# Mamba scans issued block by block in a written-out order on all engines, with the layer norm by batch

## The chip, the cores and the metric

The kernel runs on one core of one Trainium2 chip. The metric is device time in microseconds, the median of three executions. A core has five engines that run side by side: TensorE (PE, matmuls), VectorE (DVE, elementwise work and scans), ScalarE (ACT, activations), GpSimd (POOL, elementwise work) and SyncE (SP, which issues most transfers). Each takes its instructions in the order of its own queue, and waits on the others through semaphores.

## The reference, cut to what matters

The input x is 4 x 256 x 32 x 32: batch, channels, and N = 1024 positions. Layer 0 adds to x a block that starts with a group norm, a layer norm over channels, and four Mamba branches of 64 channels each; layer 1 is an attention with a mixture of 16 experts. The change concerns the Mamba branches and what leads to them:

```python
xc = xn.reshape(B, N, NB, DM).transpose(2, 0, 1, 3)          # 4 branches
...
    dA = jnp.exp(dt[..., None] * A)
    dBu = (dt * u)[..., None] * Bm[:, :, None, :]
    def step(h, inp):
        dA_t, dBu_t, C_t = inp
        h = dA_t * h + dBu_t
        return (h, jnp.einsum('bds,bs->bd', h, C_t))
...
    return ys.transpose(1, 0, 2) + u * Dp
...
return y * jax.nn.silu(z) @ outw.T                           # + skip_scale * xc
```

Here u is a short convolution and silu of the branch's input, dt a softplus of a projection of u, and B and C projections of u. Each branch has 128 inner channels with 16 states each, for 4 batches.

## The kernel before, in words

A *unit* is one branch nb in one batch b: 16 units in all. The 128 channels x 16 states of a unit don't fit on 128 partitions, so it is cut into NJ = 16 *blocks* of 8 channels x 16 states, each a tile of 128 partitions x 1024 positions. 256 blocks are scanned.

**The stages.** Part 1 loads the whole of x into four tiles X that stay for the kernel, and all weights. It takes group norm statistics of all batches (L243 to L254), then normalises batch by batch into XM (L260 by groupnorm, L213 to L226 by layernorm, L287). Then come the Mamba units. Part 2 goes over the batches with convolutions, attention, and a projection added to X. Part 3 is the second attention and the routing, part 4 the experts, and part 5 adds their results to X and stores.

**One block** (block j of the current unit `cur`) goes through all engines:

- SyncE spreads 8 rows of dt over 128 partitions into dA (L390), and ScalarE makes exp(dt x A) of it (L391).
- TensorE picks 8 rows of dt x u, spread over 128 partitions, into the PSUM tile dBu (L395). The rows are held as three bf16 parts in U.
- VectorE multiplies dBu by B (L396) and scans it with dA into hs (L398).
- GpSimd multiplies hs by C (L399).
- TensorE sums over the states into the unit's PSUM tile pY (L401).

dBu has two buffers, hs three, dA five, pY one.

**The front** of the next unit makes its u, dt, U, B and C in seven steps (a generator, one step after each block): a convolution as eight matmuls pu (L325) and a silu (L330); a projection pdt (L334) and a softplus as Abs, Relu, Exp, Identity (L339 to L342), a VectorE step (L344), Ln (L345) and a GpSimd step (L346); dt on VectorE (L348), stored to memory (L350), and dt x u on GpSimd (L352); two casts to bf16 on ScalarE (L355, L358), each with a remainder on GpSimd (L356, L359); a store dq (L361); three loads U turned to another layout (L366); and B and C as matmuls pBC (L373) with ScalarE copies (L375). All these matmuls share one PSUM tile with the tag "mm".

**The back** of a unit comes behind its 16 blocks: pz (L408) and its silu (L410), u x D + pY (L412), times silu(z) on GpSimd (L413), the output projection po (L417), and its sum into XM (L418).

The units run with nb outside and b inside. Nothing but the programming layer's scheduler sets the order of instructions on each engine: it may move an instruction ahead of or behind others where data and buffers allow.

Of the kernel before, what the change touches and what calls it, by code (L numbers as in the profile page):

```python
# [8 lines left out]
F32 = mybir.dt.float32  # L9
# [7 lines left out]
N = HH * WW  # L17
# [121 lines left out]
def body(tc, g, out):  # L139
# [8 lines left out]
    with pool("const", 1) as cp, pool("xres", 1) as xp, pool("dram", 1, space=bass.MemoryType.DRAM) as drp:  # L148
# [5 lines left out]


        X = []
        for b in range(B):
            t = xp.tile([P, CT, N], F32, tag=f"x{b}", name=f"x{b}")
            nc.sync.dma_start(out=t, in_=g["x"][b].rearrange("(t p) n -> p t n", p=P))
            X.append(t)  # L160

# [12 lines left out]

        qdw = load("qdw", [P, CT, 3 * NB])
        qpw = load("qpw", [NB, C])
        rpw = load("rpw", [P, CT, C])
        fpw = load("fpw", [P, 2 * CT, C])
        inw = load("inw", [P, CT, 3 * C])
        outw = load("outw", [P, CT, C])  # L180
        fcw = load("fcw", [P, 2 * CT, C])
        projw = load("projw", [P, CT, C])
        wq, wk, wv = (load(n, [P, CT, C]) for n in ("wq", "wk", "wv"))
        gw = load("gw", [P, CT, NE])
        rows = load("rows", [P, 2 * C + NE], g["rows"].partition_broadcast(P))
# [22 lines left out]
        def layernorm(wp, ps, src, dst):  # L208
# [5 lines left out]
            xc = wp.tile([P, CT, N], F32, tag="cm", name="xc")  # L214
            sq = wp.tile([P, CT, N], F32, tag="cm", name="sq")
# [17 lines left out]
        with pool("zero", 1) as zp:  # L233
            zero = zp.tile([P, NE * EROWS * 2 // P], F32, tag="zero", name="zero")
            nc.gpsimd.memset(zero, 0.0)
            nc.gpsimd.dma_start(out=table.rearrange("(p r) c -> p (r c)", p=P), in_=zero)

# [3 lines left out]
        with pool("gn", 2) as gp, pool("gnps", 1, space=PSUM) as gps:  # L241
            for b in range(B):
                nc.vector.tensor_reduce(sums[:, b * CT : (b + 1) * CT], X[b], AX.X, ALU.add)  # L243
            pg = gps.tile([P, B * CT], F32, tag="pg", name="pg")
            mm(pg, grp, sums, start=True, stop=True)
            nc.vector.tensor_scalar(nmean, pg, -1.0, None, ALU.mult)
            for b in range(B):
                for k in range(CT):
                    j = b * CT + k
                    junk = gp.tile([P, N], F32, tag="junk", name="junk")  # L250
                    act(junk, X[b][:, k], AF.Square, bias=nmean[:, j : j + 1], scale=1.0, accum_out=ssq[:, j : j + 1])
            pg2 = gps.tile([P, B * CT], F32, tag="pg2", name="pg2")
            mm(pg2, grp, ssq, start=True, stop=True)
            nc.vector.tensor_copy(gvar, pg2)  # L254
            rsqrt(grstd, gvar, gtmp)

        def groupnorm(dst, b):
            for k in range(CT):
                j = b * CT + k
                ts(dst[k], X[b][:, k], nmean[:, j : j + 1], grstd[:, j : j + 1], ALU.add, ALU.mult)  # L260


        with pool("xm", 1) as xmp:
# [6 lines left out]
            mcs = tc.tile_pool(name="mconst", bufs=1)  # L270
            mc = mcs.__enter__()
            m_in = load("m_in", [P, CT, 2 * DIN], where=mc)
            m_cu = mc.tile([P, CT, K, DIN], F32, tag="m_cu", name="m_cu")
            m_xp = load("m_xp", [DTR, NB, DIN], where=mc)
            m_wdt = mc.tile([P, NB, DIN], F32, tag="m_wdt", name="m_wdt")
            pick = mc.tile([96, 32 // DB, P], BF16, tag="pick", name="pick")
            m_bc = load("m_bc", [P, NB, 2 * P], where=mc)
            m_dt = load("m_dt", [DTR, NB, DIN], where=mc)
            m_out = load("m_out", [P, NB, DM], where=mc)
            with pool("lnA", 2) as wp, pool("lnAps", 2, space=PSUM) as ps:  # L280
                for b in range(B):
                    xs = wp.tile([P, CT, N], F32, tag="xs", name="xs")
                    groupnorm([xs[:, k] for k in range(CT)], b)
                    dst = [XM[b][:, k, XL : XL + N] for k in range(CT)]
                    layernorm(wp, ps, [xs[:, k] for k in range(CT)], dst)
                    for k in range(CT):
                        act(dst[k], dst[k], AF.Identity, bias=V("norm_b", k), scale=V("norm_w", k))  # L287

            aneg = cp.tile([P, NB * DS], F32, tag="aneg", name="aneg")
            act(aneg, V("alog", 0, NB * DS), AF.Exp)  # L290
            ts(aneg, aneg, -1.0, None, ALU.mult)


            with pool("convr", 1) as vp:
                convr = vp.tile([P, CT, K, DIN], F32, tag="convr", name="convr")
                nc.sync.dma_start(out=convr, in_=g["convr"])
                tt(m_cu, m_in[:, :, 0:DIN].unsqueeze(2).to_broadcast([P, CT, K, DIN]), convr, ALU.mult)
                pickf = vp.tile([96, 32 // DB, P], F32, tag="pickf", name="pickf")
                nc.sync.dma_start(out=pickf, in_=g["pick"].rearrange("k (j p) -> k j p", j=32 // DB))
                nc.vector.tensor_copy(pick, pickf)  # L300

            with pool("wdt", 1, space=PSUM) as wps:
                pw = wps.tile([P, NB, DIN], F32, tag="pw", name="pw")
                for nb in range(NB):
                    mm(pw[:, nb], m_xp[:, nb], m_dt[:, nb], start=True, stop=True)
                nc.vector.tensor_copy(m_wdt, pw)
# [4 lines left out]
            NJ = DIN // DB  # L311
            with pool("front", 1) as fp, pool("scan", 3) as sp, pool("dts", 2, space=bass.MemoryType.DRAM) as dsp, pool(
                "mps", 1, space=PSUM
            ) as mps, pool("yps", 1, space=PSUM) as yps, pool("dps", 2, space=PSUM) as dps:
                def block(nb, b):
                    q0 = (nb % 2) * DM
                    return slice(q0, q0 + DM), XM[b][q0 : q0 + DM, nb // 2]

                def front(nb, b, r):

                    rows_in, xb = block(nb, b)
                    pu = mps.tile([P, N], F32, tag="mm", name="pu")
                    for h in HALVES:
                        for k in range(K):
                            mm(  # L325
                                pu[:, h], m_cu[rows_in, nb // 2, k], xb[:, XL - K + 1 + k + h.start : XL - K + 1 + k + h.stop],
                                start=k == 0, stop=k == K - 1,
                            )
                    u = fp.tile([P, N], F32, tag="u", name="u", bufs=2)
                    act(u, pu, AF.Silu, bias=V("convb", nb), scale=1.0)  # L330
                    yield
                    pdt = mps.tile([P, N], F32, tag="mm", name="pdt")
                    for h in HALVES:
                        mm(pdt[:, h], m_wdt[:, nb, :], u[:, h], start=True, stop=True)  # L334


                    e = fp.tile([P, N], F32, tag="e", name="e")
                    dt = fp.tile([P, N], F32, tag="dt", name="dt")
                    act(e, pdt, AF.Abs, bias=V("dtb", nb), scale=1.0)  # L339
                    act(dt, pdt, AF.Relu, bias=V("dtb", nb), scale=1.0)  # L340
                    act(e, e, AF.Exp, scale=-1.0)
                    act(pdt, e, AF.Identity, bias=one, scale=1.0)  # L342
                    yield
                    stt(e, pdt, -1.0, e, ALU.add, ALU.subtract)  # L344
                    act(pdt, pdt, AF.Ln)  # L345
                    nc.gpsimd.tensor_tensor(dt, dt, e, ALU.subtract)  # L346
                    yield
                    tt(dt, dt, pdt, ALU.add)  # L348
                    ds = dsp.tile([NJ, DB, N], F32, tag="ds", name="ds")
                    nc.sync.dma_start(out=ds.rearrange("j d n -> (j d) n"), in_=dt)  # L350
                    dtu = e
                    nc.gpsimd.tensor_tensor(dtu, dt, u, ALU.mult)  # L352
                    yield
                    parts = fp.tile([P, 3, N], BF16, tag="parts", name="parts")
                    nc.scalar.copy(parts[:, 0], dtu)  # L355
                    nc.gpsimd.tensor_tensor(dtu, dtu, parts[:, 0], ALU.subtract)  # L356
                    yield
                    nc.scalar.copy(parts[:, 1], dtu)  # L358
# [594 lines left out]
```

## Time and profile before

The median of three executions is 4861.83 us (4855.08 to 4865.09); the profiled execution spans 4846.0 us.

| stretch | from, us | to, us |
|---|---|---|
| loads, statistics, layer norms, m_cu | 0 | 122 |
| first front and Mamba units | 122 | 1640 |
| part 2 (four batches) | 1640 | about 3530 |
| parts 3 to 5 | about 3530 | 4846 |

Over the span TensorE is busy 78%, VectorE 44%, ScalarE 30%, GpSimd 25%. These shares average over stages with different limits, so the stage itself is to be read. A line of the page's groups names the line, the engine, the operation, the tiles, the busy time, the mean time of one in ns, and behind the second bar the engine's idle time ahead of such instructions with what ended it.

### The profile page before, as it was taken

Reading aid. Unit: us, or ns where it says so; the run is one execution under the profiler, and the core shown is the slowest. Engines: PE = TensorE matmul, PEld = TensorE weight load, DVE = VectorE, ACT = ScalarE, POOL = GpSimd, SP = SyncE. Lnnn points to the kernel's source line nnn. Section 1 sums busy time; section 2 is a strip of 40 time slices with the busy share of each in tenths; the row PEclk is TensorE's granted clock in tenths of the full one; section 3 lists DMA queues with packets and bytes.
Section 4 is the critical chain, followed back from the end, with each engine's and each line's share of the span. In section 5 each row is a group of like instructions: output and inputs, shape, how many; then the busy total and the mean of one; then the engine's idle time right before and its main releaser. Section 6 shows DMA issues by size and latency. Waiting matters only on the chain.

```text
span 4846.0 us, 37340 instructions
## 1 busy us (share of the span) xinstructions
PE 3763.7 (78%) x14694; PEld 2010.7 (41%) x14694; DVE 2145.5 (44%) x2108; ACT 1468.9 (30%) x1864; POOL 1192.6 (25%) x738
## 2 busy tenths in 40 slices
PE   3667776767777699859985998599848776689997
PEld 1222222222222255415541554155425444478885
DVE  3366666666656544344434443544343233311112
ACT  4434434434433033313331333133322112111112
POOL 1354554555544200000000000000010122144441
PEclk8688887878878766866676668666868987799998
DMA  2443443444433000000000000000000000055554
GB/s 88 109 116 105 126 113 100 135 111 109 130 104 104 26 1 1 1 0 1 1 1 0 1 1 1 0 1 1 1 0 9 1 9 9 12 182 184 178 182 161
DMA packets 81831, 292.45 MB, mean 60 GB/s; under 512 B 13998, under 2 KB 18357, under 8 KB 75640
## 3 DMA queue, kind: packets, MB, share of 16 engines
q1 hardware_dynamic: 63272, 194.72, 14.5%
q0 software_dynamic: 18384, 95.36, 6.0%
q8 instruction: 115, 1.88, 0.2%
q14 instruction: 60, 0.49, 0.0%
HBM read 251.68 MB, written 42.27 MB: 61 GB/s over the span
## 4 chain that ended last, share of the span: by engine, by line
PE 60%; DVE 14%; POOL 10%; issue 9%; ACT 5%; DMA 2%; SPq 0%; DVEq 0%; POOLq 0%; ACTq 0%
PE sc L525 10%; PE pY L401 8%; PE pp L543 7%; PE lin L205 6%; PE p L851 6%; POOL hs L399 5%; PE po L553 4%; DVE hs L398 4%; PE po L859 3%; PE pu L325 2%; PE po L662 2%; PE sc L915 2%; PE pv L222 2%; DVE xd L613 2%; PE pm L213 1%
## 5 line engine op out<-in xcount | busy, mean ns | idle before, releaser
L401 PE MATMUL pY<-hs,const 128*128 128x512 f32 x1024 | 632.1, 762 | 180.3 <-POOL hs L399 176.6
L399 POOL TENSOR_TENSOR hs<-hs,bc 128x1024 f32<-128x1024 f32 x256 | 597.7, 2349 | 627.2 <-DVE hs L398 623.0
L525 PE MATMUL sc<-kT,qT 32*128 32x512 f32 x1024 | 575.2, 873 | 37.0 <-ACT pr L531 37.0
L398 DVE TENSOR_TENSOR_SCAN hs<-dA,dBu 128x1024 f32<-128x1024 f32 x256 | 575.5, 2274 | 18.0 <-PE pY L401 10.6
L396 DVE TENSOR_TENSOR dBu<-dBu,bc 128x1024 f32<-128x1024 f32 x256 | 304.6, 1221 | 446.1 <-PE dBu L395 445.9
L391 ACT ACTIVATE dA<-dA,aneg 128x1024 f32<-128x1024 f32 x256 | 292.8, 1147 | 592.0 <-DMA dA<-ds 588.8
L401 PEld LDWEIGHTS pY<-hs,const 128*128 128x128 f32 x1024 | 231.0, 242 | 543.8 <-POOL hs L399 309.9
L528 DVE TENSOR_REDUCE nm<-sc 128x1 f32<-128x1024 f32 x256 | 307.4, 1222 | 286.1 <-PE sc L525 286.1
L543 PEld LDWEIGHTS pp<-const,pr 128*128 128x128 f32 x2048 | 298.8, 177 | 270.4 <-issue 109.0
L226 POOL TENSOR_TENSOR xo<-xc,r 128x1024 f32<-128x1024 f32 x8 | 18.6, 2340 | 1565.9 <-DVE r L198 1565.9
L543 PE MATMUL pp<-const,pr 128*128 128x128 f32 x2048 | 377.9, 345 | 3.4 <-ACT pT L545 2.7
L531 ACT ACTIVATE pr<-sc,nm 128x1024 f32<-128x1024 f32 x256 | 286.3, 1119 | 294.0 <-DVE nm L528 293.9
L851 PE MATMUL p<-xT,w 128*128 128x256 f32 x1504 | 335.6, 381 | 9.5 <-issue 8.7
L395 PE MATMUL dBu<-U,pick 96*128 96x512 bf16 x512 | 165.6, 424 | 183.8 <-DVE hs L398 183.5
L851 PEld LDWEIGHTS p<-xT,w 128*128 128x128 f32 x1504 | 285.1, 191 | 52.4 <-ACT y L864 14.3
L545 DVE COPY pT<-pp 128x512 f32<-128x512 f32 x256 | 175.6, 686 | 231.5 <-PE pp L543 231.5
L545 ACT COPY pT<-pp 128x512 f32<-128x512 f32 x256 | 149.4, 584 | 412.2 <-PE pp L543 412.1
L854 DVE TENSOR_TENSOR hid<-s,p 128x512 f32<-128x512 f32 x94 | 64.6, 687 | 359.9 <-PE p L851 297.1
L525 PEld LDWEIGHTS sc<-kT,qT 32*128 32x128 f32 x1024 | 153.4, 242 | 168.8 <-issue 89.1
L553 PEld LDWEIGHTS po<-pT,v 128*32 128x32 f32 x4096 | 181.8, 167 | 99.0 <-issue 85.2
L553 PE MATMUL po<-pT,v 128*32 128x128 f32 x4096 | 222.0, 406 | 0.0
L859 PE MATMUL po<-w,hid 128*128 128x256 f32 x752 | 181.9, 386 | 0.0
(282 smaller groups left out, 4432.7 us busy)
## 6 DMA issues: line engine op xcount, KB each, us to landing
dA<-ds SPq DMA_DIRECT2D x256, 512.0 KB, 4.5
dq<-parts SPq DMA_DIRECT2D x16, 768.0 KB, 3.5
U<-dq SPq DMA_DIRECT2D x48, 256.0 KB, 5.7
ds<-dt SPq DMA_DIRECT2D x16, 512.0 KB, 2.6
y<-ybuf SPq DMA_DIRECT2D x32, 256.0 KB, 4.2
x<-x SPq DMA_DIRECT2D x4, 1024.0 KB, 10.3
tokens<-out_rows SPq DMA_DIRECT2D x4, 1024.0 KB, 4.5
out<-o SPq DMA_DIRECT2D x16, 256.0 KB, 2.5
```

Of the source, the lines that this page charges most:

```text
L391: act(dA, dA, AF.Exp, scale=aneg[:, nb * NJ + j : nb * NJ + j + 1])
L396: tt(dBu, dBu, cur["B"], ALU.mult)
L398: nc.vector.tensor_tensor_scan(hs, dA, dBu, 0.0, ALU.mult, ALU.add)
L399: nc.gpsimd.tensor_tensor(hs, hs, cur["C"], ALU.mult)
L401: mm(pY[:, h], strip[:, P - DB - j * DB : 2 * P - DB - j * DB], hs[:, h], start=j == 0, stop=j == NJ - 1)
L525: mm(sc[i][:, h], qT[r0 : r0 + HD, k, qs], kT[r0 : r0 + HD, k, h], start=True, stop=True)
L528: nc.vector.tensor_reduce(nm, sc[i], AX.X, ALU.max, negate=True)
L543: nc.tensor.transpose(pp[:, j * P : (j + 1) * P], pr[:, c0 : c0 + P], ident)
L545: (nc.vector.tensor_copy if half == 0 else nc.scalar.copy)(dst, pp)
L553: mm(po[i * HD : (i + 1) * HD], v[:, j, hd * HD : (hd + 1) * HD], pT[j // 4][:, i, (j % 4) * P : (j % 4 + 1) * P], start=j == 0, stop=j == ...
L851: mm(p[:, cc], w[:, o : o + P], xT[:, k], start=k == 0, stop=k == CT - 1)
L859: mm(po[:, h], hid[:, c, h * P : (h + 1) * P], w[:, o : o + C], start=c == 0, stop=c == HID // P - 1,)
```

## The change

Four things are changed, the first two in part 1. They are meant to keep every engine supplied during the scans, and to let the first scan start earlier.

**1. The scans.** The loop over blocks is written out over all 256 blocks, in a region in which each engine keeps the order of the program. In step t: product and scan of block t, times C, dBu of block t + 2, pY of block t - 2, transfer of dA for block t + 4, exponential for block t + 3; and steps of the fronts of the next two units at set places (a table of pairs: step number, function). The back of a unit is put into the next unit: gated at j = 2, project_out at j = 6, store at j = 7; gate (pz and its silu) is at j = 10 of its own unit. hs has four buffers, u three. The units run with b outside.

**2. The start.** Statistics, group norm and layer norm are done batch by batch (normalise). The first front stands behind batch 0, ahead of batches 1 to 3. m_cu and the other small tables are made at the beginning, and the weights of part 2 and later are loaded behind the layer norms.

**3. X.** The tiles X are not held during the Mamba part. x is loaded into three rotating tiles for part 1, and loaded again into X ahead of part 2.

**4. The table of the routing** is zeroed where the routing begins, through SyncE's queue, and not at the start through GpSimd's.

```diff
-        with pool("zero", 1) as zp:
-            zero = zp.tile([P, NE * EROWS * 2 // P], F32, tag="zero", name="zero")
-            nc.gpsimd.memset(zero, 0.0)
-            nc.gpsimd.dma_start(out=table.rearrange("(p r) c -> p (r c)", p=P), in_=zero)
...
+            order = [(nb, b) for b in range(B) for nb in range(NB)]
...
+                    return [(i - 5, lambda i=i: project(i)) for i in range(4)] + [
+                        (-1, silu), (0, project_dt), (1, exps), (3, rest), (4, log), (5, dt_out), (6, times_u),
+                        (8, part1), (8, lambda: spread(0)), (9, lambda: spread(1)), (10, part2), (11, turn),
+                    ]
...
+                    normalise(0)
+                    fronts = [front(n) for n in range(len(order))]
+                    for _, step in fronts[0]:
+                        step()
+                    for i, step in fronts[1]:
+                        if i < 0:
+                            step()
+                    for b in range(1, B):
+                        xs.append(load_x(b))
+                        normalise(b)
...
+                    with tc.manual_schedule():
+                        for t in range(4):
+                            fetch(t)
+                        for t in range(3):
+                            decay(t)
+                        for t in range(2):
+                            select(t)
+                        for t in range(NBLK + 9):
+                            n, j = t // NJ, t % NJ
+                            if t < NBLK:
+                                r = state[n]
+                                dBu = dBus.pop(t)
+                                tt(dBu, dBu, r["B"], ALU.mult)
+
+                                hs = hss[t] = sp.tile([P, N], F32, tag="hs", name="hs")
+                                nc.vector.tensor_tensor_scan(hs, dAs.pop(t), dBu, 0.0, ALU.mult, ALU.add)
+                                nc.gpsimd.tensor_tensor(hs, hs, r["C"], ALU.mult)
+                            if j == 2 and n > 0:
+                                gated(n - 1)
+                            select(t + 2)
+                            add_up(t - 2)
+                            fetch(t + 4)
+                            decay(t + 3)
+                            for ahead in (1, 2):
+                                if n + ahead < len(order):
+                                    for i, step in fronts[n + ahead]:
+                                        if i == j - (ahead - 1) * NJ:
+                                            step()
+                            if n > 0 and j == 6:
+                                project_out(n - 1)
+                            if n > 0 and j == 7:
+                                store(n - 1)
+                            if n < len(order) and j == 10:
+                                gate(n)
...
+            xp = late.enter_context(tc.tile_pool(name="xres", bufs=1, side="right"))
+            X = []
+            for b in range(B):
+                t = xp.tile([P, CT, N], F32, tag=f"x{b}", name=f"x{b}")
+                nc.sync.dma_start(out=t, in_=g["x"][b].rearrange("(t p) n -> p t n", p=P))
+                X.append(t)
...
+            zero = rp.tile([P, NE * EROWS * 2 // P], F32, tag="zero", name="zero")
+            nc.gpsimd.memset(zero, 0.0)
+            nc.sync.dma_start(out=table.rearrange("(p r) c -> p (r c)", p=P), in_=zero)
```

In the new code `select` is the dBu matmul, `add_up` the pY matmul, `fetch` the transfer of dA, `decay` its exponential, `turn` the transfers dq and U, `spread` the matmul and copy of B or C, and `rest`, `log`, `dt_out`, `times_u`, `part1` and `part2` are the steps of the front in their old order.

## The prediction

> **What bounds the kernel now.** I read the page's groups first, then the windows by stage, then the chain of waits and the VectorE timeline inside one turn of the scan loop.
>
> ```profile
> L401 PE MATMUL pY<-hs,const 128*128 128x512 f32 x1024 | 632.1, 762 | 180.3 <-POOL hs L399 176.6
> L398 DVE TENSOR_TENSOR_SCAN hs<-dA,dBu 128x1024 f32<-128x1024 f32 x256 | 575.5, 2274 | 18.0 <-PE pY L401 10.6
> L396 DVE TENSOR_TENSOR dBu<-dBu,bc 128x1024 f32<-128x1024 f32 x256 | 304.6, 1221 | 446.1 <-PE dBu L395 445.9
> 122.00:1640.00 1518.00, 1083.35 (x2113) 391.06 (x2114) 940.79 (x578) 596.74 (x528) 776.54 (x339) 0.81 0.41 111
> ```
>
> The window columns are length, then busy time of PE, PEld, DVE, ACT, POOL, then clock, DMA share and GB/s. The Mamba part takes 1518 us, and no engine fills it: PE 71%, DVE 62%. VectorE sits idle 446 us ahead of the dBu product, waiting for the TensorE matmul that writes dBu. The reader should see a loop of waits, not a full engine.
>
> ```profile
> 602.96 2.29 DVE hs L398
> ...
> 605.38 2.35 POOL hs L399
> ...
> 607.78 6.19 PE pY L401 x8
> 613.96 0.22 PE dBu L395
> 614.18 1.72 PE pY L401 x4
> 615.90 0.23 PE dBu L395
> ...
> 616.15 0.04 DVE dBu L396
> ```
>
> That is the chain of waits: start, duration, piece. From the scan at 602.96 the work goes to GpSimd (times C), to the pY matmuls, and only behind these to the dBu matmuls, which VectorE needs for its next blocks. TensorE's queue order puts dBu of the next blocks behind pY of these ones, so the engines take turns: 618.43 - 602.96 = 15.47 us for three blocks.
>
> ```profile
> 602.96 4.45 DVE L398 TENSOR_TENSOR_SCAN hs<-dA,dBu 128x1024 f32<-128x1024 f32 x2
> 607.33 1.21 DVE L396 TENSOR_TENSOR dBu<-dBu,bc 128x1024 f32<-128x1024 f32 x1
> 608.67 2.29 DVE L398 TENSOR_TENSOR_SCAN hs<-dA,dBu 128x1024 f32<-128x1024 f32 x1
> 616.15 2.36 DVE L396 TENSOR_TENSOR dBu<-dBu,bc 128x1024 f32<-128x1024 f32 x2 [5.20 <-PE dBu L395]
> 663.08 1.23 DVE L396 TENSOR_TENSOR dBu<-dBu,bc 128x1024 f32<-128x1024 f32 x1 [1.74 <-PE dBu L395]
> 664.22 1.21 DVE L348 TENSOR_TENSOR dt<-dt,pdt 128x1024 f32<-128x1024 f32 x1
> 665.35 2.28 DVE L398 TENSOR_TENSOR_SCAN hs<-dA,dBu 128x1024 f32<-128x1024 f32 x1
> 667.54 2.34 DVE L396 TENSOR_TENSOR dBu<-dBu,bc 128x1024 f32<-128x1024 f32 x2
> ```
>
> From this timeline I take the VectorE spacings: a scan starts 1.34 us after the product it needs (607.33 to 608.67); whatever follows a scan starts 2.19 us after it (665.35 to 667.54); an independent elementwise operation takes 1.13 to 1.14.
>
> ```profile
> 568.00:572.00 4.00, 2.29 (x7) 0.97 (x6) 4.00 (x3) 1.96 (x2) 4.00 (x2) 1.00 0.46 131
> 604.00:608.00 4.00, 0.83 (x3) 0.34 (x4) 4.00 (x3) 0.00 (x0) 2.62 (x2) 0.75 0.36 97
> 608.00:612.00 4.00, 4.00 (x5) 1.63 (x6) 2.82 (x2) 1.19 (x2) 2.93 (x2) 0.50 0.67 165
> ```
>
> These short windows show the clock. It stays at 1.00 while TensorE is busy 57% with gaps of 1.7 us; after a pause of 4.2 us (ahead of the dBu matmul at 605.29) it is 0.50. Weight loads in the timeline come every 0.427 us at full clock and 0.853 at half, so a 128x512 f32 matmul (two records) is 0.85 or 1.71 us.
>
> **What the Trainium skill says.** "TensorE: Matmul & The Clock Gate", section "What's actually happening": the clock is halved after an idle window of about 3.4 us and restored after a busy one. The windows above agree. The same page, "Architectural detail: the array is 16× 32×32, not 1× 128×128", says that ScalarE, VectorE and GpSimd run strictly in order, so a waiting instruction holds all behind it; I rely on this below. "ScalarE: Activation LUTs", section "What ACT_TABLE_LOAD costs": 1283 ns plus a drain of about 1380. The trace has the 1283 ns (20.5 us for 16 loads); the exp table load ends at 162.85 and the exponential starts at 162.87, so no further drain is seen and I use 1.28. "DMA: Bandwidth & Descriptors", section "Two DMAs through the same engine are not ordered": a transfer that reads what another writes needs its completion. The trace agrees: U is issued at 166.97, 4.1 us after dq at 162.87.
>
> **The change, part by part.**
>
> *Order of the scans.* A unit is one (nb, b) of 16, with 16 blocks. In the written order TensorE computes dBu two blocks ahead and pY two blocks late. The dBu matmul of block t+2 needs only the end of scan t, which frees its buffer, and has until the end of scan t+1. pY finds its input long ready. So VectorE should run product, scan, product, scan: 1.34 + 2.19 = 3.53 us per block, 256 x 3.53 = 904 us. Per unit it also has the softplus rest (1.13), dt (1.14), gated (1.20 by 626.85 to 628.05) and store (1.32 by 633.26 to 634.58): 4.79, in 15 units 72.
>
> *Can the other engines keep up?* TensorE at full clock: 0.43 (dBu) + 1.71 (pY) = 2.14 us in each block, and in nine of 16 (j = 0, 6, 8 to 14) another 1.71 for a projection: 3.85. Seven such blocks in a row lag 7 x 0.32 = 2.2 us behind VectorE, inside the block of slack that dBu has (3.53 less 0.5). In sum 16 x 2.14 + 9 x 1.71 = 50 us of about 64; gaps are at most 1.4 us, so I take the clock as full. GpSimd: 16 x 2.35 + 3 x 2.35 + 2 x 2.13 = 49. ScalarE: 16 x 1.15 + silus, exps, log, casts, copies (11 operations, 11.6) + six table loads of 1.28 = 38. DMA: 105 to 129 GB/s over units of 95 us becomes about 165 at 64 us; single 4 us windows reach 307. None fills the unit.
>
> *Waits that the order adds on VectorE.* dt (j = 5) is queued ahead of product 6. It needs GpSimd's dt - e, which is queued behind hs of block 4: scan 4's end + 2.35 + 2.35 = 4.7, while VectorE is there after 3.53: 1.2 us. store (j = 7) needs project_out, which ends 0.43 + 1.71 + 1.71 + 0.3 after scan 6: 0.6 us. Each is paid 15 times: 18 and 9 us.
>
> *The turn (j = 11).* SyncE issues dq when GpSimd has parts (scan 10's end + 5.9, since ScalarE waits for spread in j = 8 and 9), waits about 4.1 for its landing, then issues U three times in 1.3; U lands 5.6 later: about 16.2 after scan 10. The first dBu of the next unit is due by scan 15 (5 x 3.53 = 17.7): it fits by about 1 us. Behind U stand the fetches of dA from block 16 on: issued at about 11, landed with 4.5 to 8.1 us behind U's traffic at 16 to 19, exponential 1.15; due at 5 x 3.53 + 1.34 = 19.0. This is between no wait and some 3 us; I take 1.5 a unit, 22 in all. Table loads and the single "mm" buffer make ScalarE late by up to a block, but each step has one or two blocks of slack, the tightest (exps of j = 1 ahead of rest at j = 3) about 0.9 us.
>
> Sum from the first to the last scan: 904 + 72 + 18 + 9 + 22 = 1025 us. The tail: hs 2.4, pY 1.9, gated 1.3, times sz 2.35, po 1.9, store 1.3 = 11.
>
> *The start.* Before, the first scan starts at 185.7: statistics of all batches to 31.8, four layer norms to 119, m_cu at 121, then front 0 alone (122 to 182). Now batch 0 has statistics at about 18 (x lands at about 8, then 2.3 for the sum, 2.3 of squares, some 5 of table loads and small steps) and is normalised 26.6 later, as its first layer norm took from 31.8 to 58.4; front 0 then runs beside batches 1 to 3, which take 20 us each (52.4, 72.5, 92.8 between GpSimd steps): 45 + 60 = 105. For sharing ScalarE (about 75 us of work and loads in this stretch) I add 10. The scan tiles lie in the freed memory, so the first fetch comes at about 115, and 4.5 + 1.15 later the first scan: 122. I take 107 to 150 as ends.
>
> *What costs nothing.* Weight loads move behind the layer norms; SyncE is idle there. X is read again (4 MB): room is free when the last hs is used, some 7 us before the tail ends, and X is first used at 1661.30, 21 us after part 2 begins; a load of 1 MB took 10.3. The zero fill of the table goes from the start to the routing: a 1 us memset and 512 KB, hidden by the attention ahead of the first scatter. Parts 2 to 4 otherwise keep their instructions.
>
> New end of the Mamba part: 122 + 1025 + 11 = 1158, against 1639.7 now: 481 us less. From the median, 4861.8 - 481 = 4380 us.
>
> **The rivals.**
>
> *TensorE at half clock.* If the pattern doesn't hold the clock, each unit needs 16 x 4.27 + 9 x 3.41 = 99 us, TensorE is the bound, and the part ends at 122 + 1584 + 13 = 1719: 79 us later than now, 4941 us. For it: clock 0.81 now. Against it: at half clock TensorE would have no gap, and full windows bring 1.00. This ends on the slower side.
>
> *SyncE's queue becomes the bound.* If U or the dA behind it come 4 to 8 us late per unit instead of 1.5, that is 40 to 100 us more: 4420 to 4480. For it: margins of 1 us in the turn. Against it: four dA are in flight ahead.
>
> *Clock in between (0.8).* TensorE needs 50 / 0.8 = 62 us a unit; its lag beats its slack in the dense blocks, 3 to 6 us a unit: 4430 to 4480.
>
> *No waits at all and a short start.* 107 + 976 + 11 = 1094: 546 less, 4316.
>
> **How the numbers follow.** My forecast (4335 to 4420) has 0.62, SyncE's queue 0.16, a clock in between 0.09, no waits 0.08, half clock 0.04, and 0.01 for a cancelling loss in the rescheduled later parts. The likeliest time is 4380. The range goes down to 4310, for the short start, and up to 4490, for the SyncE and clock cases. Faster by over 0.2% 0.95, within 0.2% 0.01, slower 0.04.
>
> **What would show it.** Scans 3.5 us apart with no wait for dBu; VectorE over 90% busy in the scan stretch; clock 0.95 or more there; first scan near 122, last near 1145; unit length near 64; waits of dt on GpSimd of 1.2 and of store on po of 0.6. Wrong if scans wait for dA after each j = 11, or TensorE shows 0.5 with no gaps, or the first scan comes after 150.

## The result, and the profile after

The changed kernel takes 4451.86 us in the median of four executions (4440.12 to 4459.88), beside 4858.45 us for the kernel before on the same chip. The ratio is 0.9161, with a 95% interval of 0.9136 to 0.9187. The forecast was 4380 us: the gain is 407 us where 481 were worked out. The profiled execution spans 4438.3 us, and its parts are these:

| | before, us | forecast, us | after, us |
|---|---|---|---|
| start of the first scan | 185.7 | 122 | 139.8 |
| from there to the start of the last scan | 1436 | 1023 | 1073.6 |
| end of the last store of the Mamba part | 1639.7 | 1158 | 1228.5 |
| from there to the end of the span | 3206 | 3206 | 3210 |

So the 72 us that are missing are 18 at the start, 51 between the scans, and a few in the rest. The later parts are as long as before, to 4 us. X is loaded again at 1220.21 and first used at 1247.00, with no wait for it.

First the page's groups of the kernel after; behind the first bar stand busy time and mean ns, behind the second the idle time ahead of such instructions and what ended most of it:

```profile
L476 DVE TENSOR_TENSOR_SCAN hs<-dA,dBu 128x1024 f32<-128x1024 f32 x256 | 585.4, 2287 | 81.9 <-PE pY L459 49.7
L459 PE MATMUL pY<-hs,const 128*128 128x512 f32 x1024 | 532.9, 646 | 14.3 <-DVE u L342 12.5
L473 DVE TENSOR_TENSOR dBu<-dBu,bc 128x1024 f32<-128x1024 f32 x256 | 311.6, 1217 | 1.7 <-PE dBu L451 1.6
```

The idle time ahead of the dBu product, 446 us before, is 1.7: the loop of waits is gone. A pY record takes 646 ns, 762 before, since the clock is higher. In place of the old wait stands a smaller one that the forecast had at nothing: the scan waits 49.7 us for pY, which has to release the hs buffer that the scan writes.

The windows of the kernel after (length; busy time of PE, PEld, DVE, ACT, POOL; clock, DMA share, GB/s): the scans, then one stretch of dense blocks (blocks in which TensorE has a projection besides dBu and pY) and two behind pauses of TensorE.

```profile
138.00:1216.00 1078.00, 885.50 (x2055) 343.33 (x2056) 953.18 (x571) 565.36 (x511) 764.63 (x331) 0.93 0.59 153
604.00:608.00 4.00, 4.00 (x11) 1.54 (x10) 3.35 (x3) 0.00 (x0) 3.11 (x2) 1.00 1.04 221
640.00:644.00 4.00, 3.00 (x5) 1.45 (x5) 3.90 (x3) 1.15 (x1) 2.91 (x2) 0.60 0.75 215
651.00:655.00 4.00, 3.34 (x5) 1.48 (x6) 3.87 (x3) 0.00 (x0) 3.25 (x2) 0.51 0.51 124
```

In the scan stretch VectorE is busy 88% (62% before) and the clock is 0.93 (0.81 before). It is 1.00 in the stretch of dense blocks shown, and near a half in the two short ones.

The waits of VectorE in the scan stretch of the kernel after (the instruction that waited, what for; us in total, times, longest):

```profile
DVE hs L476 <- PE pY L459: 49.7, 79, 1.6
DVE xm L356 <- PE mm L350: 29.5, 15, 2.4
DVE dt L292 <- POOL dt L289: 18.5, 15, 1.2
DVE hs L476 <- ACT dA L444: 9.8, 1, 9.8
DVE dBu L473 <- PE dBu L451: 1.6, 3, 0.6
```

Beside hs waiting for pY these are store (L356), waiting for project_out; dt (L292), waiting for GpSimd; one wait of 9.8 for the very first dA, which belongs to the start; and almost nothing for dBu. Three terms make up the stretch from first to last scan. From start to start there are 255 spacings of 3.53 us, 900 us; the extras (the four VectorE operations of a unit that are no part of a block: gated, rest, dt and store) are 72, as forecast; and the waits are 49.7 + 29.5 + 18.5 + 1.6 = 99.3. That makes 1072, against 1073.6 measured. Where the waits come from is seen in TensorE's timeline; the columns are start, duration, engine, line, and in brackets the idle time ahead:

```profile
600.82 0.60 PE L451 MATMUL dBu<-U,pick 96*128 96x512 bf16 x2
601.26 1.88 PE L459 MATMUL pY<-hs,const 128*128 128x512 f32 x4
603.07 1.98 PE L263 MATMUL mm<-xm,m_cu 64*128 64x512 f32 x4
604.98 0.60 PE L451 MATMUL dBu<-U,pick 96*128 96x512 bf16 x2
...
641.00 1.01 PE L451 MATMUL dBu<-U,pick 96*128 96x512 bf16 x2 [3.68 <-DVE hs L476]
641.80 3.10 PE L459 MATMUL pY<-hs,const 128*128 128x512 f32 x4
644.83 1.93 PE L350 MATMUL mm<-u,m_out 128*64 128x512 f32 x4
...
658.61 0.60 PE L451 MATMUL dBu<-U,pick 96*128 96x512 bf16 x2
659.05 1.88 PE L459 MATMUL pY<-hs,const 128*128 128x512 f32 x4
660.76 1.88 PE L320 MATMUL mm<-u,m_bc 128*128 128x512 f32 x4
662.48 0.60 PE L451 MATMUL dBu<-U,pick 96*128 96x512 bf16 x2
```

A dense block with a 128-row projection takes 662.48 - 658.61 = 3.87 us, and the forecast had 3.85. One with the 64-row convolution (L263) takes 604.98 - 600.82 = 4.16, without a gap and at full clock: pY is 1.81 from start to start and the convolution 1.91, where the first has 1.71 and 1.72. Of the seven dense blocks of a unit, five are of the 64-row kind (j = 10 to 14). In the middle, TensorE pauses 3.68 us in the block of j = 5 and runs at half clock behind it, so that the projection that store needs comes late. VectorE's timeline of the same turns:

```profile
607.51 2.29 DVE L476 TENSOR_TENSOR_SCAN hs<-dA,dBu 128x1024 f32<-128x1024 f32 x1 [0.65 <-PE pY L459]
...
611.68 2.29 DVE L476 TENSOR_TENSOR_SCAN hs<-dA,dBu 128x1024 f32<-128x1024 f32 x1 [0.65 <-PE pY L459]
...
636.19 1.22 DVE L292 TENSOR_TENSOR dt<-dt,mm 128x1024 f32<-128x1024 f32 x1 [1.23 <-POOL dt L289]
...
646.80 1.27 DVE L356 SCALAR_TENSOR_TENSOR xm<-xm,vec,mm 64x1024 f32<-64x1024 f32 x1 [2.34 <-PE mm L350]
```

Scans in a row of 64-row blocks are 611.68 - 607.51 = 4.17 us apart, TensorE's pace, with 0.65 of waiting each time. The 79 waits for pY in the list are about five in each of the 16 units, most of them at j = 13 to 15, 0 and 1.

The waits of store show what the clock does. Of the 15, eleven are 2.3 to 2.4 us and four are 0.72 to 0.75, close to the 0.6 of the forecast. One of the four, a unit later (TensorE, then VectorE):

```profile
710.80 0.59 PE L451 MATMUL dBu<-U,pick 96*128 96x512 bf16 x2 [3.27 <-DVE hs L476]
711.23 1.88 PE L459 MATMUL pY<-hs,const 128*128 128x512 f32 x4
...
715.01 1.29 DVE L356 SCALAR_TENSOR_TENSOR xm<-xm,vec,mm 64x1024 f32<-64x1024 f32 x1 [0.75 <-PE mm L350]
```

The same pY takes 1.88 us here and 3.10 at 641.80. Here the half clock came earlier, and was over when TensorE reached the block of project_out, though it had paused 3.27 us ahead of that.

### The profile page after: what moved, and what is told of

Same layout as the page of the kernel before. It is cut to its first block, busy times and chain, and to the rows that moved or that the text cites. A ratio compares the mean times of both kernels' runs of the same rounds, so it can differ in the third digit from the quotient of the medians.

```text
span 4438.3 us, 37207 instructions
## 1 busy us (share of the span) xinstructions
PE 3600.0 (81%) x14706; PEld 1973.7 (44%) x14706; DVE 2176.5 (49%) x2123; ACT 1460.9 (33%) x1872; POOL 1193.8 (27%) x737
## 3 DMA queue, kind: packets, MB, share of 16 engines
q8 instruction: 115, 1.88, 0.2%
## 4 chain that ended last, share of the span: by engine, by line
PE 66%; DVE 15%; POOL 5%; ACT 4%; issue 4%; DMA 2%; SPq 0%; DVEq 0%; POOLq 0%; ACTq 0%
PE sc L606 11%; PE pp L624 7%; PE pY L459 7%; PE p L935 7%; PE lin L188 6%; PE po L634 5%; PE po L943 4%; DVE hs L476 3%; PE po L746 2%; PE sc L999 2%; PE mm L263 2%; PE dBu L451 2%; PE pv L205 2%; DVE xd L694 2%; POOL hs L477 2%
## 5 line engine op out<-in xcount | busy, mean ns | idle before, releaser
L476 DVE TENSOR_TENSOR_SCAN hs<-dA,dBu 128x1024 f32<-128x1024 f32 x256 | 585.4, 2287 | 81.9 <-PE pY L459 49.7
L459 PE MATMUL pY<-hs,const 128*128 128x512 f32 x1024 | 532.9, 646 | 14.3 <-DVE u L342 12.5
L209 POOL TENSOR_TENSOR xo<-xc,r 128x1024 f32<-128x1024 f32 x8 | 18.6, 2340 | 1563.5 <-DVE r L181 1563.5
L459 PEld LDWEIGHTS pY<-hs,const 128*128 128x128 f32 x1024 | 209.2, 206 | 204.0 <-issue 166.8
L451 PEld LDWEIGHTS <-pick 96*128 96x128 bf16 x512 | 42.1, 99 | 381.7 <-issue 303.1
```

Of the source, the lines that this page charges most:

```text
L451: mm(dBus[t][:, h], pick[:, j % 4], state[t // NJ]["U"][:, j // 4, h], start=True, stop=True)
L459: mm(r["pY"][:, h], strip[:, P - DB - j * DB : 2 * P - DB - j * DB], hs[:, h], start=j == 0, stop=j == NJ - 1)
L476: nc.vector.tensor_tensor_scan(hs, dAs.pop(t), dBu, 0.0, ALU.mult, ALU.add)
```

## The experiments

There are three theories on the missing 51 us between the scans: TensorE's pace in the dense blocks, where hs is freed late; SyncE's queue around the turn, the rival of the prediction; and the pauses around dt and store. A fourth question is how much of the gain comes from the order in which instructions are handed out, and how much from holding every engine to it. All times at a glance, with the first-to-last-scan time of each trace:

| kernel | median, us | ratio to before (95%) | first to last scan, us |
|---|---|---|---|
| before | 4858 | 1 | 1436 |
| after | 4452 | 0.9161 (0.9136 to 0.9187) | 1074 |
| e1_dt_late | 4394 | 0.9044 (0.9030 to 0.9058) | 1021 |
| e2_hs6 | 4447 | 0.9153 (0.9132 to 0.9175) | 1072 |
| e3_free_order | 4330 | 0.8913 (0.8863 to 0.8963) | 965 |
| e4_two_taps | 4455 | 0.9172 (0.9146 to 0.9199) | 1091 |
| e5_gate7 | 4383 | 0.9044 (0.9012 to 0.9076) | 1013 |
| e6_split_turn | 4390 | 0.9055 (0.9030 to 0.9081) | 1022 |
| e7_taps_split | 4412 | 0.9093 (0.9056 to 0.9130) | 1045 |
| e8_free_plain | 4766 | 0.9820 (0.9795 to 0.9845) | 1347 |
| e9_three | 4376 | 0.9031 (0.9011 to 0.9051) | 1006 |
| e10_free_front1_late | 4327 | 0.8938 (0.8917 to 0.8959) | 967 |
| e11_between | 4393 | 0.9068 (0.9047 to 0.9090) | 1022 |
| e12_free_dbu_only | 4432 | 0.9137 (0.9111 to 0.9164) | 1045 |

The kernel before was run beside each group of experiments, with medians of 4844 to 4858; so kernels of different groups are compared by their ratios.

**e1: dt one block later.** The step dt_out goes from j = 5 to j = 6.

```diff
-(3, rest), (4, log), (5, dt_out), (6, times_u),
+(3, rest), (4, log), (6, dt_out), (6, times_u),
```

> dt_out moves from j = 5 to j = 6, one block later; the same work. Theory (waits on VectorE, and the pause they give TensorE): the wait of dt on GpSimd (18.5 us in 15 times) goes to about 0; TensorE's pause of 3.7 us at j = 5 shrinks under 3, so its clock stays full and the wait of store on project_out (29.5 us) falls under 5; in sum 40 to 50 us less than the changed kernel's 4452, about 4405. Rival (TensorE's whole work sets the unit's length): what is saved comes back as longer waits of the scan on pY, the time stays within 10 us of 4452.

The waits of VectorE in the scan stretch of e1:

```profile
DVE hs L476 <- PE pY L459: 48.3, 81, 1.1
...
DVE xm L356 <- PE mm L350: 0.7, 1, 0.7
```

The dt wait is gone, and with it all but 0.7 us of the store wait, which the edit doesn't touch: 47 us of waits out, 52 us less from first to last scan. So the two were one. VectorE's block of j = 5 took 3.53 + 1.14 + 1.2 = 5.87 us, and TensorE, with 2.14 of work there, paused for the rest of it, 3.73 (3.68 in the trace), and then ran at half clock. But the clock did not stay full, as the theory had it: between 150 and 1100 us it is 0.95, beside 0.94 in the changed kernel. The half clock has moved to other blocks, away from project_out: in e1 a pause of 2.36 us ahead of 607.10 is followed by a pY of 3.17 us. The waits for pY stay, so they have another cause.

**e2: six hs buffers in place of four.**

```diff
-hs = hss[t] = sp.tile([P, N], F32, tag="hs", name="hs")
+hs = hss[t] = sp.tile([P, N], F32, tag="hs", name="hs", bufs=6)
```

> hs gets six buffers in place of four; the same work. Theory (in blocks j = 8 to 14 TensorE itself needs 4.17 us a block and sets the pace; dBu of the block is due from it almost as early as the buffer): VectorE gains only some 0.4 us a unit, 0 to 10 us in all, and waits for dBu appear where waits for pY were. Rival (too few hs buffers): the 49.7 us of waits of the scan on pY go, 40 to 50 us less.

The scan's waits for pY are gone, and in the waits of VectorE of e2 there stands instead:

```profile
DVE dBu L473 <- PE dBu L451: 32.4, 67, 0.6
```

The time is that of the changed kernel, as the theory had it. The buffers only decide where VectorE waits for TensorE; the pace is TensorE's.

**e4: two of the four taps of the convolution left out.** (A tap is one of the four shifted inputs that are multiplied and summed.) The parts at j = 12 and 14 are then empty, and TensorE has 3.8 us less to do in the dense blocks.

```diff
-for k in range(part % 2 * 2, part % 2 * 2 + 2):
-    mm(..., start=k == 0, stop=k == K - 1)
+for k in range(2) if part % 2 == 0 else ():
+    mm(..., start=k == 0, stop=k == 1)
```

> Leaves out two of the four taps of the convolution (half of the matmuls of pu), so that blocks j = 12 and 14 have no projection on TensorE. Theory (a dense run of seven blocks at 4.17 us against VectorE's 3.54 builds up a lag of 4.4 us, over the slack of about 3): the lag stays under the slack, waits of the scan on pY fall from 50 to under 15, 35 to 45 us less than 4452. Rival (hs buffers or another wait): waits on pY stay over 30.

No gain, where 35 to 45 us were expected, though the waits of VectorE in e4 show that the scan's wait for pY fell from 49.7 to 18.6. From first to last scan e4 is even 17 us longer than the changed kernel; its first scan comes 8 us earlier, at 132.1. The waits:

```profile
DVE u L342 <- PE pY L459: 41.7, 14, 5.9
...
DVE hs L476 <- PE pY L459: 18.6, 30, 0.7
```

A new wait of 41.7 us, of gated (L342) for pY, took its place. Its source is found by following the releasers back. TensorE's timeline in e4, at the first projection of the next unit (project_dt, which needs the silu of u):

```profile
620.04 1.98 PE L274 MATMUL mm<-u,m_wdt 128*128 128x512 f32 x4 [2.22 <-ACT u L267]
```

and ScalarE's ahead of it:

```profile
614.16 1.15 ACT L444 ACTIVATE dA<-dA,aneg 128x1024 f32<-128x1024 f32 x1 [1.08 <-DMA dA<-ds]
616.41 1.15 ACT L444 ACTIVATE dA<-dA,aneg 128x1024 f32<-128x1024 f32 x1 [1.10 <-DMA dA<-ds]
617.58 1.28 ACT L267 ACT_TABLE_LOAD   x1
618.87 1.11 ACT L267 ACTIVATE u<-mm,vec 128x1024 f32<-128x1024 f32 x1
```

The exponentials wait for dA; the silu stands behind them on ScalarE, project_dt behind the silu, and behind project_dt on TensorE the pY that gated needs. The dA stand behind dq and U in SyncE's queue: U is issued at 603.86, and the next dA only at 605.23. So SyncE's queue may be a second limit, right behind TensorE's; e7 tries that.

**e7: e4 with the turn split.** If that is so, the three loads U, which wait for dq to land and hold all behind them, must not be issued at once. The step turn issues dq at j = 11, and a new step back issues U at j = 12, so that a fetch of dA goes between. The two taps are left out here too.

```diff
-(10, part2), (11, turn),
+(10, part2), (11, turn), (12, back),
```

> Leaves out two of the four taps of the convolution, as in the run with two taps, and splits the turn over j = 11 and 12; dt_out at j = 5. Theory (with the dense run thinned, SyncE's queue was what held ScalarE, then project_dt and pY at the unit's start): the wait of gated on pY, 41.7 us, falls under 10, and the time falls to about 4410. Rival (that wait has another source on ScalarE or TensorE): within 10 us of 4455.

Two of the waits of VectorE in e7:

```profile
DVE hs L479 <- PE pY L462: 17.3, 25, 2.3
DVE u L345 <- PE pY L462: 5.4, 2, 4.5
```

Gated's wait (L345 here) for pY fell from 41.7 to 5.4, and first to last scan by 46 us. With two taps left out, then, SyncE's queue was the limit, and what lies between e4 and e7 was its own: 0.9172 - 0.9093 of 4858, or 38 us (two executions each; the intervals don't meet). The dt and store waits are still in e7, since dt_out is at j = 5 in it.

**e6: the split turn on e1, with all taps.** The same edit as in e7, on top of e1's.

> dt_out at j = 6 as before, and the loads of U move from j = 11 to j = 12, behind the transfer of dA of block j + 4, so that this transfer doesn't stand behind the landing of dq. Theory (TensorE's dense run is the binding limit there, the queue of SyncE the next one): ScalarE's 8 us wait for dA shortens, but the time stays within 10 us of 4394. Rival (SyncE's queue sets the unit already): 20 to 40 us less.

4390 beside 4394, and the interval of the ratio covers e1's: no gain that could be told from none. The scan still waits 46.6 us for pY, as in e1. ScalarE's longest wait for dA fell, from 8.1 to 5.5 us, as expected. The edit that frees SyncE's queue paid with two taps and pays nothing here: with the full convolution TensorE is the first limit.

**e5: gate earlier.** pz, one of the 64-row projections, goes from j = 10 to j = 7, out of the dense blocks; on top of e1's edit.

```diff
-if n < len(order) and j == 10:
+if n < len(order) and j == 7:
     gate(n)
```

> dt_out at j = 6 as before, and gate (the pz matmul and its silu) moves from j = 10 to j = 7, so that TensorE's dense run of seven blocks becomes two runs of four. Theory (the dense run's lag makes the waits of the scan on pY, 48 us): each run's lag stays under the slack, the waits fall under 20 us, 20 to 30 us less than 4394. Rival (ScalarE's order: the silu at j = 7 holds the casts of parts behind it, and U comes later): waits move to gated or to dBu at the unit's start, 0 to 20 us more than 4394.

The waits of VectorE in e5:

```profile
DVE u L342 <- PE pY L459: 25.1, 15, 4.5
DVE hs L476 <- ACT dA L444: 21.5, 14, 9.5
DVE hs L476 <- PE pY L459: 2.8, 4, 1.7
```

The wait for pY ahead of the scan is nearly gone (48.3 to 2.8), so it has to do with the run of dense blocks. But the edit does two things: it takes a projection out of the run, and it fills TensorE's pause at j = 7. The clock between 150 and 1100 us is 0.98, beside 0.95 in e1, and the block of j = 8, the first of the long run, takes 3.86 us where it takes 5.58 in most units of e1, at half clock. How the two share the effect was not tried. And as in e4, other waits come forward: gated waits 25.1 and the scans 12 us for dA (9.5 of the 21.5 are the start). First to last scan is 8 us shorter than in e1, where 20 to 30 were expected; the times don't settle it, since the intervals overlap.

**e9: all three, dt late, gate at j = 7 and the split turn.**

> Fixed order with three moves together: dt_out at j = 6, gate at j = 7, the loads of U at j = 12. Theory (with dt and the dense run mended, the queue of SyncE is the last limit: in the run with gate at j = 7, waits of 25 us of gated on pY and of 12 us on dA came from it): these waits fall under 10 in sum, about 4355. Rival (the turn isn't what holds the unit's start): within 10 us of 4383.

The waits of VectorE in e9 (line numbers are 3 higher):

```profile
DVE hs L479 <- PE pY L462: 23.4, 30, 2.1
DVE hs L479 <- ACT dA L447: 9.6, 1, 9.6
DVE dBu L476 <- PE dBu L454: 6.2, 8, 1.4
```

The waits of gated, and those for dA but for the one of the start, are gone. But the scan's waits for pY, 2.8 in e5, are 23.4, half of e1's 48.3; so in e5 the other waits had hidden a part of them. The 4355 expected became 4376. A cause that the waits of VectorE don't show stands in TensorE's own waits, between 150 and 1100 us of e9:

```profile
PE dBu L454 <- DMA U<-dq: 16.3, 13, 3.6
```

With U issued a block later, TensorE itself waits for U at the end of 13 units (9.9 us in e5, none in e1). How much of the 23.4 comes from this was not tried. By its median e9 is the fastest of the kernels that hold the written order, though its interval overlaps those of e1, e5 and e6.

**e11: e9 with the extras between product and scan.** The scan starts 1.34 us after its product, an independent operation after 1.13. So gated, rest and dt_out were put into that place, at j = 2, 4 and 7 (with times_u behind dt_out), to use the 0.2 us.

```diff
 tt(dBu, dBu, r["B"], ALU.mult)
+if j == 2 and n > 0:
+    gated(n - 1)
...
 hs = hss[t] = sp.tile([P, N], F32, tag="hs", name="hs")
```

> The three moves, and gated, rest and dt_out put between a block's product and its scan (at j = 2, 4 and 7), where VectorE has a gap of 0.2 us between the two. Theory: 0.2 us for each of three operations in 15 units, 5 to 15 us less than the run with the three moves. Rival (the operations put there delay the scan and what GpSimd and ScalarE do with their results): the same or up to 20 us more.

The rival came true: e11 is 18 us slower than e9. The largest of VectorE's waits in e11:

```profile
DVE u L345 <- PE pY L462: 36.7, 15, 2.9
```

VectorE comes to gated a scan earlier, before the pY of the unit is summed, and waits for it in all 15 units. A place that saves 0.2 us cost 2.4.

**e3: the written order as a program only.** The region that holds each engine to it is taken away (contextlib.nullcontext() in place of it), and the scheduler may move instructions again. Nothing else differs from the changed kernel.

```diff
-with tc.manual_schedule():
+with contextlib.nullcontext():
```

> The region of fixed order is taken away: the same instructions are emitted in the same order, but the scheduler may move them on each engine. Theory (the order on TensorE's queue is what brought the gain): the scheduler ranks pY and dBu its own way, waits of VectorE on dBu return in part, 4500 to 4750. Rival (emitting dBu two blocks ahead and pY two behind, with b outside, is enough): within 20 us of 4452.

4330 us, about 120 less than the changed kernel, whose interval of the ratio lies wholly above; neither theory nor rival had expected a gain. The four executions lie between 4303 and 4354 us, so the 120 are known to some 25. VectorE's timeline in e3:

```profile
639.49 1.21 DVE L473 TENSOR_TENSOR dBu<-dBu,bc 128x1024 f32<-128x1024 f32 x1
640.60 1.27 DVE L342 SCALAR_TENSOR_TENSOR u<-u,vec,pY 128x1024 f32<-128x1024 f32 x1
641.79 2.28 DVE L476 TENSOR_TENSOR_SCAN hs<-dA,dBu 128x1024 f32<-128x1024 f32 x1
...
652.86 2.34 DVE L473 TENSOR_TENSOR dBu<-dBu,bc 128x1024 f32<-128x1024 f32 x2
655.11 4.46 DVE L476 TENSOR_TENSOR_SCAN hs<-dA,dBu 128x1024 f32<-128x1024 f32 x2
659.60 1.29 DVE L356 SCALAR_TENSOR_TENSOR xm<-xm,vec,mm 64x1024 f32<-64x1024 f32 x1
```

and the largest of its waits:

```profile
DVE hs L476 <- PE pY L459: 25.1, 37, 1.6
```

The scheduler did by itself what the hand order lacks. On GpSimd it put the step that dt needs ahead of the product with C of block 4, not behind it, so that dt stands between product and scan of block 5, earlier than in the written order, and doesn't wait; the store wait is gone too. It put 43 extras between a product and its scan. And in 57 places it runs two products and then two scans: 659.60 - 652.86 = 6.74 us for two blocks, where the written order takes 7.06. The clock between 150 and 1100 us is 0.98 in e3 and 0.94 in the changed kernel. The 109 us from first to last scan come about: 18.5 + 29.5 of waits gone, 24.6 less for pY, and (965 - 72 - 32 of waits) / 255 = 3.38 us a block, which is 39 less than 255 x 3.53; that makes 112, of which new waits for dA take 3. Of the 39, the pairs are about 57 x 0.32 = 18 and the extras in the gaps 43 x 0.2 = 9; the rest was not divided.

**e8: free, and without working ahead.** The scheduler is free as in e3, and dBu and pY of block t are both written in step t; gated moves to j = 0. dA stays ahead.

```diff
-for t in range(2):
-    select(t)
...
+    select(t)
     if t < NBLK:
...
-    select(t + 2)
-    add_up(t - 2)
+        add_up(t)
```

> No region of fixed order, and dBu and pY of block t emitted in step t itself, gated at j = 0; fetch, decay and the fronts stay ahead as they are. Theory (emitting dBu ahead and pY behind is what ranks them rightly for the scheduler): VectorE waits for dBu again, 4500 to 4700. Rival (b outside, the fronts two units ahead, the back inside the next unit and more buffers brought the gain): within 30 us of 4330.

4766, more than even the theory expected: of the 407 us of the change only 87 are left (1.8%). The largest of VectorE's waits in e8:

```profile
DVE dBu L474 <- PE dBu L451: 323.1, 72, 9.8
```

It is the old loop of waits, with new buffers, new order of units and new start around it.

**e12: free, with dBu two blocks ahead, but pY in step t.** As in e8, gated is at j = 0, which the lines below don't show.

```diff
     select(t + 2)
-    add_up(t - 2)
+    if t < NBLK:
+        add_up(t)
```

> Free order; dBu emitted two blocks ahead as in the change, but pY of block t in step t itself, behind dBu of block t + 2, and gated at j = 0. Theory (what counts is that dBu of the next blocks ranks ahead of pY of this one): within 30 us of 4330. Rival (pY has to be emitted late too, since in step t it stands in TensorE's queue waiting for GpSimd): waits of VectorE on dBu return, 4450 to 4750.

The largest of VectorE's waits in e12:

```profile
DVE dBu L473 <- PE dBu L451: 76.0, 70, 3.2
```

4432 is neither within 30 us of 4330 nor above 4450: the waits for dBu return, as the rival had it, but smaller. dBu ahead is worth 0.9820 - 0.9137 = 6.8% of the time before, about 332 us. pY two blocks late on top of it, together with gated at j = 2 in place of 0, is worth 0.9137 - 0.8913 = 2.2%, about 109; the two were not tried apart.

**e10: e3 with a shorter start.** The four convolution parts and the silu of the second unit (i < 0) stand ahead of the layer norms of batches 1 to 3 in the changed kernel; here they stand behind them.

```diff
-for i, step in fronts[1]:
-    if i < 0:
-        step()
 for b in range(1, B):
     xs.append(load_x(b))
     normalise(b)
+for i, step in fronts[1]:
+    if i < 0:
+        step()
```

> Free order as before, and the convolution and silu of the second unit (front 1, eight matmuls, 7.1 us on TensorE) put behind the layer norms of all batches. Theory (TensorE's in-order queue holds the last layer norms behind it, and the first dA waits for their memory): the first scan comes 5 to 10 us earlier than 146.9, the time falls by as much. Rival (ScalarE's chain of table loads sets the layer norms): no earlier scan.

The first scan comes at 138.8 and not 146.9, and the last 6 us earlier. In the time it can't be told from e3 (the intervals overlap). It has the lowest median of all, 4327. It is about 10.6% faster than the kernel before, and by the ratios (0.9161 - 0.8938, of 4858 us) about 108 us faster than the changed one.

## Why the prediction was right, and where it was off

The time lies in the range of 4310 to 4490, and the mechanism came true: the loop of waits for dBu was the bound, and working ahead removes it (446 us of waits became 1.6). What was off are sizes, by 72 us in sum. That the total still lies in the range is in part luck: 4452 is outside the 4335 to 4420 of the likeliest case, and the upper end had been put there for other cases. Of these, SyncE's queue as the bound didn't come: no scan but the first waits for dA. The clock in between came by half: TensorE's lag does beat its slack in the dense blocks, by 3.1 us a unit where 3 to 6 were told, but the clock in most of them is full.

Of the signs that were told, the missing waits for dBu and the dt wait of 1.2 us came. VectorE at 88% (over 90 told), the clock of 0.93 (0.95), the first scan at 139.8 (122), 67 us a unit (64) and 2.0 us of store wait in the mean (0.6) did not; none of the signs of being wrong came.

- **Spacing of 3.53 us, and extras of 72.** Right for the written order. The trace has about 3.5 where nothing waits, and the sum of these and the measured waits meets the measured stretch within 2 us. But the kernel before ran pairs in places, two products and then two scans, at 6.65 us for two blocks (from the product at 600.68 to the one at 607.33). The written order gives this up, which the forecast did not price; e3 has it again.
- **dt wait, 18.** Right in place and size, 18.5. What it drags behind it was not seen.
- **store wait, 9.** The term was mis-sized: 29.5. The step that failed is "gaps are at most 1.4 us, so I take the clock as full". The 1.4 is for a block without an extra. The blocks of j = 5 and 7 have an extra on VectorE and no projection on TensorE, so TensorE pauses 3.68 and 2.65 us, and the clock is 0.60 and 0.51 behind them. In eleven of 15 units the block of project_out runs into the half clock; in the other four the wait is 0.72 to 0.75, about as forecast. e1 removed the dt wait alone, and the store wait went with it.
- **Dense blocks at 3.85 us, whose lag of 2.2 fits a slack of about 3.** This term, taken as 0, was the largest: 49.7. The 128-row blocks are 3.87, but the five 64-row ones are 4.16, since I had priced every projection by the 128-row pY matmul; so the lag is 2 x 0.34 + 5 x 0.63 = 3.8 us a unit at full clock. And the run often begins late: its first block, j = 8, takes up to 6.95 us (651.66 to 658.61) at half clock, 3.1 more than the 3.87. The slack was counted for dBu, while hs comes first; with six hs buffers (e2) waits for dBu stand in their place, and the time is the same. The waits are 49.7 / 16 = 3.1 us a unit. How much of the lag the buffers took up, and how much of the waits comes from the shapes and how much from the late beginning, was not measured apart; e5 changes both and has nearly none of these waits, e9 half of them.
- **The turn, 22.** None of it is seen on VectorE: the margin of dA held, as the forecast's own lower end had it. That SyncE's queue is near its limit was right, as e4 and e7 show. It is a limit behind TensorE's, and comes forward once TensorE is relieved; and the margin of U, some 1 us, is used up in e9, where TensorE waits for U.
- **The start, 122.** It was 139.8, within its ends of 107 to 150. The term for sharing (10 us) was too small. The layer norms of batches 1 to 3 share ScalarE and TensorE, which work in order, with the first front and the convolution of the second: VectorE waits 14.48 us for a layer norm's pm at 108. e10, where the second unit's steps stand behind the norms, starts its scans 8 us earlier than e3, and e4, with half of the convolution left out, 8 us earlier than the changed kernel. How the rest divides was not tried.
- **X again, weights, zero fill at nothing.** In line with it: from the end of the Mamba part on 3210 us, 3206 before. None of them was tried alone.
- **What the experiments add to the argument.** The gain was put down to the written order. e3 and e8 divide that: working ahead (with gated at j = 2) is worth about 440 us, and holding the engines to this order takes about 120 of it away again. A better order by hand, e9, wins about half of that back. The forecast said nothing on this second half.

## What to carry to other kernels

Where engines wait for each other in a circle, hand out the producer's work a few steps ahead and the consumer's a few behind, before anything else; then try a free schedule too, since it can show where a strict order by hand costs waits of its own, as e3 does here. In a fixed order, price each block's work for each engine by the shapes that it has, and lay steps so that no block leaves an engine idle and none has more than the pace, since a wait on one engine comes back on another. A fix that gains nothing may have met a second limit just behind the first: read which wait has grown before you drop it.

## What the runs showed of the hardware

- The clock of TensorE goes by fixed windows here, and not by the length of a pause. In the trace of the changed kernel it is 1 or a half, and all its changes lie on one grid of 3.413 us. Counted over its windows between 200 and 1100 us, with the ends of matmuls as the profile models them: all 30 at full clock in which TensorE was busy 40% or less were followed by half clock, and none of the 200 in which it was busy more. So where a pause falls decides. A pause of 2.37 us ahead of 701.27 (busy 1.04 of the 3.41 us from 698.85 on) was followed by half clock; one of 3.27 us ahead of 710.80 was split over two windows (busy 1.70 of the 3.41 us from 709.09 on), and the clock stayed full. The Trainium skill, "TensorE: Matmul & The Clock Gate", section "What's actually happening", has the clock fall after an idle window of about 3.4 us, and lets the windows run free of the kernel. The grid agrees; that the window has to be idle does not, and the measurement decides. The 40% is no general limit: in e3 some windows with TensorE busy for half of the time and more were followed by half clock.
- f32 matmuls over 64 rows between others over 128 rows take more than those over 128 rows throughout: 4.16 us in place of 3.87 for the same number of matmuls of 512 columns at full clock. The trace has the whole difference at the changes: from start to start it is 0.52 to 0.53 us for the last record ahead of a change and for the first behind the change to 64 rows, and 0.43 for the others, as in the 128-row blocks (604.98 to 609.15).
